# Cross-attention and feed-forward on one core: group 0's divisions on ScalarE, output weights' loads ahead of sums, first weights loaded by column halves

## The chip, the cores and the metric

The kernel runs on one core of one Trainium2 chip. The metric is the time of one execution on the device, in microseconds (us). The core has five engines that run their own queues of instructions in order: TensorE (PE in the profile; PEld is its load of weights), VectorE (DVE), ScalarE (ACT), GpSimd (POOL) and SyncE (SP). Transfers are issued from SyncE's, ScalarE's and GpSimd's queues.

## The reference, cut to what matters

There are 8 batches of 128 rows, a width of 512, 32 heads of width 128, and an inner feed-forward width of 1376. All is float32.

```
h     = rmsnorm(layernorm(x)) * ln_weight          # 8 x 128 x 512
q     = h @ w_q.T;  k = ctx @ w_k.T;  v = ctx @ w_v.T     # 32 heads of 128
score = softmax(where(mask, q k^T + position_bias, -inf)); 0 where masked
att   = (score @ v), heads side by side            # 8 x 128 x 4096
x     = x + layernorm(x) + att @ w_out.T
g     = layernorm(x)
x     = x + (silu((g @ Wg.T) * ag) * ((g @ Wu.T) * au)) @ Wd.T * ad
```

Two sequences in the softmax matter here: the exponentials with their row sums, and the division of each row by its sum.

## The kernel before

**Groups, batches, and products with fewer multiplications.** The 32 heads are worked in 8 groups of 4 (`NG`, `GH`), so a group's weights are 512 columns (`GW`). Most matrix products are done in a scheme of seven products of half-sized blocks in place of eight (`seven`, `inner`, `four`): the operands are split into quarters, sums of quarters are formed ahead (`sums_a`, `sums_b`, `combine_rows`, `token_sums`), TensorE multiplies, and ScalarE copies or VectorE adds each product into its result. So each weight needs four sums on GpSimd before all of its products can run, but the first two products read weights that are in no sum.

**The start.** The first group's weights of k and v (`wk0`, `wv0`) and the transposed context (`ctx_sb`) come from HBM; each tile holds 4 chunks of 128 rows. Lines 152 to 162 issue them: chunks 2 and 3 of k and of the context's first 512 tokens one by one, then v, then the rest in halves (`load_part`), ScalarE's queue and SyncE's queue in parallel. The context's other 512 tokens come last, in two parts. `first_kv` (566) then runs the products of k and v of group 0 in the order of 570 to 589: two products of k's blocks (number 2), two of v's, then number 1 of each, then those that read sums. `ctx_sums(0)` to `ctx_sums(3)` are the token sums on VectorE and GpSimd. In the same loop (682) x is normalised on VectorE and ScalarE. Then the queries of all groups are projected and stored to HBM (741 to 772).

**The groups.** From line 888 on, group g's attention runs batch by batch, while the k and v of the next group are projected between the batches (`later_kv`). `probabilities` (495) does a batch of a group: 4 matmuls of scores into one bank (`sc`, one buffer); VectorE adds the masked bias that GpSimd has made (`masked_bias`, 490), takes the rows' maxima and negates them (506 to 510); ScalarE takes 4 exponentials with sums (515); VectorE inverts the sums (522, 523) and multiplies (526), writing the columns in another order, so that every fourth element of `s` is read. `transpose_p` (533) turns the result by a VectorE transposition of 32x32 blocks and a way through HBM on SyncE's queue. Three batches later `attend` (547) multiplies it by v, and ScalarE copies the product out and stores it to HBM (556, 557).

Where an engine is wrapped in `InOrder`, its instructions keep the order of the program (all such have line 62 in the profile). Otherwise a scheduler may set them in another order. Group 0 is in order for batches 0 to 3, group 7 throughout.

**The last group** (line 900 on). There is no next group, so TensorE works on the output projection meanwhile: in pass b it does batch b's scores, an older batch's product with v, and the output products of group b-1 for rows of batches 0 and 1 (`out_products`, `out_product`). For these, VectorE forms sums of the attended rows (`att_sums`, in `between`), and GpSimd sums of the output weights (`sums` in `load_wo`). `load_wo(g)` issues the weights' load on GpSimd's queue where g > 2, and returns the function that does the sums. In a pass GpSimd first makes the masked bias of batch b+2 (which waits for the division of batch b-1, whose tile it takes over), then does the sums of the weights whose load was issued at the end of the pass before (930), and at the end of the pass the next load is issued (987, 988). Group 7's weights go into two tiles of their own (791, 792). After the loop, TensorE finishes group 7's output products (1000), begins those of the next two batches' rows (1001), and so on to the residual, the second norm and the feed-forward part.

Of the kernel before, what the change touches and what calls it, by code (L numbers as in the profile page):

```python
# [17 lines left out]
P = 128  # L18
BS = 32
# [47 lines left out]
def xattn_ffn_kernel(  # L67
# [19 lines left out]
    nc = tc.nc  # L87
# [5 lines left out]
    GH = 4  # L93
    NG = H // GH
    GW = GH * P
# [5 lines left out]
    HW = GW // 2  # L101
# [41 lines left out]
    wk0 = wpool.tile([P, DC, GW], F32, tag="w", name="wk0")  # L143
    wv0 = wpool.tile([P, DC, GW], F32, tag="w", name="wv0")

    def load_part(eng, t, src, fh, cols=slice(None)):
        eng.dma_start(
            t[:, bass.ts(fh, HC), cols],
            src[bass.ts(fh, D // 2), cols].rearrange("(c p) n -> p c n", p=P),
        )  # L150

    g0 = slice(0, GW)
    for c in (2, 3):
        nc.scalar.dma_start(wk0[:, c], wkT[bass.ts(c, P), g0])
        nc.sync.dma_start(ctx_sb[:, c, :512], ctxT[bass.ts(c, P), :512])
    for c, eng in ((2, nc.scalar), (3, nc.sync)):
        eng.dma_start(wv0[:, c], wvT[bass.ts(c, P), g0])
    load_part(nc.scalar, wk0, wkT[:, g0], 0)
    load_part(nc.sync, ctx_sb, ctxT, 0, slice(0, 512))
    load_part(nc.scalar, wv0, wvT[:, g0], 0)  # L160
    for fh in (1, 0):
        load_part(nc.sync, ctx_sb, ctxT, fh, slice(512, T))
    kv_w = {0: (wk0, wv0)}
# [1 line left out]
    for b in range(B):  # L165
        nc.sync.dma_start(x_in[b // 2][:, b % 2, :], x[b])

    vector, gpsimd, scalar, sync = (
        InOrder(tc, e) for e in (nc.vector, nc.gpsimd, nc.scalar, nc.sync)
    )  # L170
# [324 lines left out]
    def probabilities(g, b, qT, kT, pb, between=None, s=None, ahead=None):  # L495

        cols = bass.ts(b, S)
        n = f"{g}_{b}"
        if s is None:
            s = masked_bias(gpsimd, g, b, pb)  # L500
        sc = ps.tile([P, GH, S], F32, tag="sc", name=f"sc_{n}")
        for j in range(GH):
            tensor.matmul(  # L503
                sc[:, j, :], qT[:, j, bass.ts(b % 2, S)], kT[j][:, cols], start=True, stop=True
            )
        vector.tensor_tensor(s, sc, s, ALU.add)
        mx = small.tile([P, GH], F32, tag="mx", name=f"mx_{n}")
        vector.tensor_reduce(mx, s, AX.X, ALU.max)
        nmx = small.tile([P, GH], F32, tag="nmx", name=f"nmx_{n}")
        vector.tensor_scalar(nmx, mx, FLOOR, -1.0, ALU.max, ALU.mult)  # L510
        sm = small.tile([P, GH], F32, tag="sm", name=f"sm_{n}")
        if ahead:
            ahead()
        for j in range(GH):
            scalar.activation(  # L515
                s[:, j, :], s[:, j, :], AF.Exp,
                bias=nmx[:, j : j + 1], accum_out=sm[:, j : j + 1],
            )
        if between:
            between()  # L520
        ri = small.tile([P, GH], F32, tag="ri", name=f"ri_{n}")
        vector.tensor_scalar_max(ri, sm, TINY)
        vector.reciprocal(ri, ri)

        p = work.tile([P, GH, S], F32, tag="p", name=f"p_{n}", bufs=1)
        vector.tensor_tensor(  # L526
            p.rearrange("q h (j r) -> q h j r", r=BS), s.rearrange("q h (r j) -> q h j r", r=BS),
            ri.unsqueeze(2).unsqueeze(3).to_broadcast([P, GH, 4, BS]), ALU.mult,
        )
        return p  # L530
# [151 lines left out]
    for n, _ in enumerate(first_kv()):  # L682
        if n in moments_at:
            pair[moments_at[n]] = norm1_moments(moments_at[n])
        if n in scales_at:
            b = scales_at[n]
# [6 lines left out]
        if n in turns_at:  # L693
            b = turns_at[n]
# [14 lines left out]
    scalar = nc.scalar  # L709
# [31 lines left out]
    for g in range(NG):  # L741
# [4 lines left out]
        w, heads = combine_rows(f"q{g}", q_w.pop(g)) if g else rows_q, []  # L746
# [26 lines left out]
    gpsimd = nc.gpsimd  # L773
# [114 lines left out]
    for g in range(NG):  # L888
        kT, v = kvs.pop(g)
        pb = biases.pop(g)  # L890
        if g + 1 < NG:
            biases[g + 1] = load_bias(g + 1)
        if g + 2 < NG:
            kv_w[g + 2] = load_kv(g + 2)
        if g == 0:
            products = later_kv()
        if g == NG - 2:
            wo_later = Later()
            load_wo(2)(wo_later)
        if g == NG - 1:  # L900
            tensor, vector = InOrder(tc, nc.tensor), InOrder(tc, nc.vector)
            fetched, next_fetched = {}, {}
            gpsimd, sync, wo_sums = InOrder(tc, nc.gpsimd), InOrder(tc, nc.sync), None
            biased = [masked_bias(gpsimd, g, k, pb) for k in range(2)]

            bulk = InOrder(tc, nc.scalar)
            come[1, 0] = load_att(1, 0, bulk)
        for b in range(B):
            if (g, b) == (NG - 2, B - 1):
                come = {(0, 0): load_att(0, 0, nc.sync)}  # L910
            if b % 2 == 0:
                qT = ahead.pop((g, b // 2))
                at = todo.index((g, b // 2)) + 2
                if at < len(todo):
                    ahead[todo[at]] = load_queries(*todo[at], nc.sync if g + 1 < NG else bulk)

            if (g, b) == (0, 0):
                tensor = kv_tensor = InOrder(tc, nc.tensor)
                vector, scalar, gpsimd = (
                    InOrder(tc, e) for e in (nc.vector, nc.scalar, nc.gpsimd)  # L920
                )
                done = next(products) + next(products)
            if g == NG - 1:


                if b + 2 < B:
                    biased.append(masked_bias(gpsimd, g, b + 2, pb))
                for _ in range(2):
                    wo_later.next(gpsimd)
                if wo_sums:  # L930
                    wo_sums = wo_sums(gpsimd)

                def between():
                    if b == 0:
                        next(products)
                    fetched[b] = att_sums(b, 0, come.pop((b, 0)), vector)

                p = probabilities(g, b, qT, kT, pb, between, biased.pop(0))
            elif g == 0 and b < 4:
                def one():  # L940
                    nonlocal done
                    done += next(products)

                if b == 0:
                    biased = [masked_bias(gpsimd, g, k, pb) for k in range(2)]
                biased.append(masked_bias(gpsimd, g, b + 2, pb))
                p = probabilities(g, b, qT, kT, pb, one, biased.pop(0), one)
            elif g == 0 and b < 6:
                p = probabilities(g, b, qT, kT, pb, s=biased.pop(0))
            else:  # L950
                p = probabilities(g, b, qT, kT, pb)
                if g == NG - 2:
                    for _ in range((0, 1, 1, 1, 1, 2, 2, 2)[b]):
                        wo_later.next(InOrder(tc, nc.gpsimd))
            pend.append((g, b, transpose_p(g, b, p), v))
            advance(3)

            if g == NG - 1:
                while next(products, None):
                    pass  # L960
            else:
                while done < due(g, b):
                    done += next(products)
            if (g, b) == (NG - 2, 2):

                sums.close()
                wos = pools(outp)("wosA", 2, side="right", reuse_waits="tile")
                load_wo(0)(wo_later)
                load_wo(1)(wo_later)
            if (g, b) == (0, 3):  # L970
                tensor, vector, scalar = nc.tensor, nc.vector, nc.scalar
                kv_tensor = tensor
            if (g, b) == (1, B - 1):
                gpsimd = nc.gpsimd
            if g == NG - 1:
                if b == 0:
                    proj.close()
                    wos = pools(outp)("wosB", 2, reuse_waits="tile")

                    first_banks = [  # L980
                        pl.tile([P, 2, HW], F32, tag=tag, name=f"m{k}_0")
                        for k, (pl, tag) in enumerate(2 * [(ps_mm, "mm")] + 2 * [(ps_b, "i")])
                    ]
                    first_out = out_products(0, list(range(NG)), first_banks, fetched)
                n = (b + 2) % B, (b + 2) // B
                come[n] = load_att(*n, bulk)
                if b < NG - 3:
                    wo_sums = load_wo(b + 3)
                if b:
                    next(first_out)  # L990
                if b + 2 >= B:
                    next_fetched[n[0]] = att_sums(*n, come.pop(n), gpsimd)


    scalar = InOrder(tc, nc.scalar)
# [15 lines left out]
    vector, gpsimd = nc.vector, nc.gpsimd  # L1011
# [78 lines left out]
    scalar = nc.scalar  # L1090
# [120 lines left out]
    for i in range(NP):  # L1211
# [9 lines left out]
        if i == 0:  # L1221
            wd = load_down()

            gpsimd = InOrder(tc, nc.gpsimd)
# [162 lines left out]
```

## Time and profile before

| | us |
|---|---|
| median of 3 runs | 1087.78 |
| lowest and highest | 1086.01, 1088.52 |
| the profiled execution | 1089.21 |
| its span, first to last instruction | 1087.4 |
| TensorE busy | 1074.8 |
| VectorE busy | 659.4 |
| ScalarE busy | 331.7 |
| GpSimd busy | 442.5 |
| mean granted TensorE clock | 0.999 |

How to read it: the profile is one execution, with times in us from its first instruction. In a timeline each line is a start, a duration, the engine, the line of the kernel, the operation, output<-inputs, shapes and a count; in brackets stands how long the engine was idle before it and what ended that. TensorE's float32 matmuls appear as two records for each instruction. In the list of waits each line is the engine and what it did, what it waited for, the total in us, the times and the longest. In the chain of waits each line is a start, a duration and what was being done or waited for. The groups of instructions have the count and, after the bar, the busy time in us, the mean of one in ns, and the idle time before them. In five-us stretches, VectorE is busy 4.37 us from 15 to 20 and 4.86 us from 20 to 25, and not at all from 10 to 15. From 240 to 320, which is nearly all of group 0, TensorE is busy 75.94 us of 80, VectorE 66.63 and ScalarE 36.16.

### The profile page before, as it was taken

How to read it: one execution, taken by the hardware profiler on the slowest of the kernel's cores; microseconds unless marked ns; L12 is line 12 of the kernel's file. 1: busy time of each engine (PE TensorE's matmuls, PEld its weight loads, DVE VectorE, ACT ScalarE, POOL GpSimd, SP SyncE). 2: the span in 40 equal slices, each digit the busy share in tenths (PEclk: the TensorE clock that was granted, in tenths of full speed). 3: DMA queues.
4: the chain of work that ended last, by engine and by line, in shares of the span. 5: the costliest groups of instructions: out<-in, count | busy, mean ns of one | idle time of the engine just before them, and what ended most of it. 6: DMA issues, size and time to landing. Idle time of an engine off the chain costs nothing.

```text
span 1087.4 us, 13761 instructions
## 1 busy us (share of the span) xinstructions
PE 1074.8 (99%) x4802; PEld 790.5 (73%) x4802; DVE 659.4 (61%) x1219; ACT 331.7 (31%) x902; POOL 442.5 (41%) x488
## 2 busy tenths in 40 slices
PE   9999999998999999999999999999999999999998
PEld 5656666556869788887879778978888864444787
DVE  4653443447888888888787767854544242544732
ACT  2633223214544444444444343311000012233100
POOL 6233554624565545555551444561000317920010
PEclk9999999999999999999999999999999999999999
DMA  9613344453755465454645657673442622110011
GB/s 290 194 53 117 116 172 170 161 207 122 243 185 194 161 199 182 135 199 153 217 165 189 214 183 225 237 263 110 173 136 78 194 80 77 39 39 1 1 39 39
DMA packets 124692, 161.80 MB, mean 149 GB/s; under 512 B 15600, under 2 KB 77296, under 8 KB 124624
## 3 DMA queue, kind: packets, MB, share of 16 engines
q1 hardware_dynamic: 110208, 129.73, 36.1%
q10 hardware_dynamic: 12544, 24.38, 6.3%
q0 software_dynamic: 1872, 6.82, 2.0%
q8 instruction: 38, 0.62, 0.2%
q14 instruction: 30, 0.25, 0.1%
HBM read 104.81 MB, written 56.10 MB: 148 GB/s over the span
## 4 chain that ended last, share of the span: by engine, by line
PE 86%; DVE 7%; DMA 3%; issue 2%; ACT 2%; POOL 0%; SPq 0%; ACTq 0%; DVEq 0%; POOLq 0%
PE mm_f L1229 11%; PE mm_q L453 10%; PE m L834 9%; PE mm_v L474 8%; PE mm_k L453 8%; PE d L1308 6%; PE i_q L402 6%; PE m L62 5%; PE i_v L415 5%; PE i_k L402 4%; PE av L551 4%; PE sc L503 4%; PE mm_v L62 2%; PE mm_k L62 1%; PE mm_q L62 1%
## 5 line engine op out<-in xcount | busy, mean ns | idle before, releaser
L515 ACT ACTIVATE s<-s,nmx 128x128 f32<-128x128 f32 x240 | 93.4, 390 | 69.5 <-DVE nmx L510 51.8
L492 POOL TENSOR_TENSOR s<-pb,mneg 128x512 f32<-128x512 f32 x40 | 50.8, 1271 | 128.5 <-DVE p L526 110.4
L397 DVE TENSOR_TENSOR q<-q,i_q 128x512 f32<-128x512 f32 x98 | 49.9, 550 | 82.1 <-PE i_q L402 81.7
L556 ACT COPY aT<-av 128x512 f32<-128x512 f32 x60 | 35.1, 585 | 144.9 <-PE av L551 113.9
L526 DVE TENSOR_TENSOR p<-s,ri 128x512 f32<-128x512 f32 x52 | 64.2, 1235 | 1.4
L503 PEld LDWEIGHTS sc<-k,q 128*128 128x128 f32 x416 | 54.0, 192 | 8.3 <-issue 6.7
L376 ACT COPY q<-mm_q 128x512 f32<-128x512 f32 x56 | 31.4, 587 | 93.8 <-PE mm_q L453 66.6
L453 PE MATMUL mm_q<-hT,wq 128*128 128x512 f32 x128 | 58.5, 592 | 0.0
L62 POOL TENSOR_TENSOR s<-pb,mneg 128x512 f32<-128x512 f32 x24 | 30.4, 1270 | 66.9 <-DVE p L526 41.0
L474 PE MATMUL mm_v<-wv,ctx_sb 128*128 128x256 f32 x240 | 56.2, 380 | 0.7 <-ACT v L345 0.7
L453 PE MATMUL mm_q<-hT,S_q 128*128 128x512 f32 x120 | 55.9, 592 | 0.0
L503 PE MATMUL sc<-k,q 128*128 128x128 f32 x416 | 55.4, 275 | 0.0
L551 PE MATMUL av<-pT,v 128*128 128x128 f32 x416 | 55.0, 275 | 0.0
L474 PE MATMUL mm_v<-S_v,ctx_sb 128*128 128x256 f32 x232 | 54.7, 380 | 0.3 <-ACT v L376 0.2
L453 PE MATMUL mm_k<-ctx_sb,wk 128*128 128x512 f32 x112 | 52.6, 593 | 0.0
L62 POOL TENSOR_TENSOR S_q<-wq 128x512 f32<-128x512 f32 x8 | 10.1, 1268 | 104.2 <-ACT wq L62 104.2
L397 DVE TENSOR_TENSOR v<-v,i_v 128x512 f32<-128x512 f32 x84 | 43.9, 541 | 11.6 <-PE i_v L415 11.1
L551 PEld LDWEIGHTS av<-pT,v 128*128 128x128 f32 x416 | 50.6, 192 | 0.1
L62 PE MATMUL m<-wo,a 128*128 128x256 f32 x200 | 49.3, 382 | 1.3 <-DMA wo<-in_woT_dram 0.9
L474 PEld LDWEIGHTS mm_v<-wv,ctx_sb 128*128 128x128 f32 x240 | 44.8, 190 | 6.5 <-ACT v L345 0.9
L453 PE MATMUL mm_k<-ctx_sb,S_k 128*128 128x512 f32 x104 | 48.6, 593 | 0.0
L834 PE MATMUL m<-wo,a 128*128 128x256 f32 x200 | 48.4, 379 | 0.0
(327 smaller groups left out, 2465.2 us busy)
## 6 DMA issues: line engine op xcount, KB each, us to landing
queries<-q SPq DMA_DIRECT2D x32, 512.0 KB, 3.9
turned<-tt SPq DMA_DIRECT2D x64, 256.0 KB, 2.8
pT<-turned SPq DMA_DIRECT2D x64, 256.0 KB, 3.0
att<-aT ACTq DMA_DIRECT2D x64, 256.0 KB, 2.9
q<-queries SPq DMA_DIRECT2D x30, 512.0 KB, 5.1
a<-att SPq DMA_DIRECT2D x23, 512.0 KB, 4.3
wq<-in_wqT_dram SPq DMA_DIRECT2D x8, 1024.0 KB, 6.9
wk<-in_wkT_dram SPq DMA_DIRECT2D x7, 1024.0 KB, 5.4
```

The lines of the kernel that those rows point to most:

```text
L62: return self.tc.keep_in_program_order(getattr(self.engine, op)(*args, **kw))
L397: vector.tensor_tensor(to, to, out, ADD)
L402: kv_tensor.matmul(out, a[n][i], b[n][i], start=first, stop=True, skip_group_check=True)
L453: kv_tensor.matmul(out, w[i][:, c, bass.ts(t, P)], src[i][:, c, :], start=(first and c == 0), stop=(c == HC - 1), skip_group_check=True,)
L474: kv_tensor.matmul(out[:, bass.ts(k, HW)], src[i][:, c, bass.ts(2 * t + k, S)], w[i][:, c, :], start=(first and k == 0 and c == 0), stop=( ...
L503: tensor.matmul(sc[:, j, :], qT[:, j, bass.ts(b % 2, S)], kT[j][:, cols], start=True, stop=True)
L515: scalar.activation(s[:, j, :], s[:, j, :], AF.Exp, bias=nmx[:, j : j + 1], accum_out=sm[:, j : j + 1],)
L526: vector.tensor_tensor(p.rearrange("q h (j r) -> q h j r", r=BS), s.rearrange("q h (r j) -> q h j r", r=BS), ri.unsqueeze(2).unsqueeze(3). ...
L551: tensor.matmul(av[:, j, :], v[b // 2][:, b % 2, bass.ts(j, P)], pT[:, :, j, :], start=True, stop=True,)
L834: tensor.matmul(m[n], sa[n][:, c, :], wo_t[g][n][:, c, :], start=(g == order[0] and c == 0 and PRODUCTS.index(n) % 2 == 0), stop=(g == ord ...
L1229: nc.tensor.matmul(out, ws[t][n][:, c, :], h2_t[n][:, :, c, :], start=(first and c == 0), stop=(c == HC - 1), skip_group_check=True,)
L1308: nc.tensor.matmul(out, lhs, rhs, start=bank not in started, stop=(i == NP - 1 or n == 8), skip_group_check=True,)
```

## The change

Three things are changed.

1. The first weights of k and v are loaded by halves of their columns: the left 256 columns of the chunks that the first products read come first (k's by chunk, then v's, then the other row halves), and both right halves follow in one transfer each. The transfers of the context keep their order, but on SyncE's queue v's left half of rows 0 to 255 and v's right half now stand ahead of its last two.
2. In group 0 the division is done by four ScalarE multiplications, one for each head of the group, in place of one VectorE operation. The reading and writing order stays.
3. In the last group, the load of group b+3's output weights is issued in pass b after the bias, ahead of the sums of those of group b+2. It was issued at the end of the pass. As the first load (group 3) is still issued at the end of pass 0, the sums begin in the same pass as before.

```
-    g0 = slice(0, GW)
+    left, right = slice(0, HW), slice(HW, GW)
     for c in (2, 3):
-        nc.scalar.dma_start(wk0[:, c], wkT[bass.ts(c, P), g0])
+        nc.scalar.dma_start(wk0[:, c, left], wkT[bass.ts(c, P), left])
         nc.sync.dma_start(ctx_sb[:, c, :512], ctxT[bass.ts(c, P), :512])
-    for c, eng in ((2, nc.scalar), (3, nc.sync)):
-        eng.dma_start(wv0[:, c], wvT[bass.ts(c, P), g0])
-    load_part(nc.scalar, wk0, wkT[:, g0], 0)
+    load_part(nc.scalar, wv0, wvT, 1, left)
     load_part(nc.sync, ctx_sb, ctxT, 0, slice(0, 512))
-    load_part(nc.scalar, wv0, wvT[:, g0], 0)
+    load_part(nc.scalar, wk0, wkT, 0, left)
+    load_part(nc.sync, wv0, wvT, 0, left)
+    for eng, w, src in ((nc.scalar, wk0, wkT), (nc.sync, wv0, wvT)):
+        eng.dma_start(w[:, :, right], src[:, right].rearrange("(c p) n -> p c n", p=P))
     for fh in (1, 0):
         load_part(nc.sync, ctx_sb, ctxT, fh, slice(512, T))
...
         p = work.tile([P, GH, S], F32, tag="p", name=f"p_{n}", bufs=1)
+        if g == 0:
+            for j in range(GH):
+                scalar.mul(
+                    p[:, j].rearrange("q (j r) -> q j r", r=BS),
+                    s[:, j].rearrange("q (r j) -> q j r", r=BS), ri[:, j : j + 1],
+                )
+            return p
         vector.tensor_tensor(
...
-            gpsimd, sync, wo_sums = InOrder(tc, nc.gpsimd), InOrder(tc, nc.sync), None
+            gpsimd, sync = InOrder(tc, nc.gpsimd), InOrder(tc, nc.sync)
...
-                if wo_sums:
-                    wo_sums = wo_sums(gpsimd)
+                if 0 < b < NG - 3:
+                    wo_todo.append(load_wo(b + 3))
+                if b and wo_todo:
+                    wo_todo.pop(0)(gpsimd)
...
-                if b < NG - 3:
-                    wo_sums = load_wo(b + 3)
+                if b == 0:
+                    wo_todo = [load_wo(b + 3)]
```

## The prediction

> **What bounds the kernel now.** I read the page's busy shares, then who waited for whom on TensorE, then the timeline in the three places that the diff touches.
>
> ```profile
> PE 1074.8 (99%) x4802; PEld 790.5 (73%) x4802; DVE 659.4 (61%) x1219; ACT 331.7 (31%) x902; POOL 442.5 (41%) x488
> ```
>
> TensorE is busy for 1074.8 of 1087.4 us, and no part of the change removes a matmul. So the most that it can win is idle time of TensorE, 12.6 us and the little that pipelined durations hide. Its longest waits, in us:
>
> ```profile
> PE i_k L62 <- DVE k L62: 2.0, 1, 2.0
> PE i_k L402 <- POOL s L62: 1.0, 1, 1.0
> PE m L62 <- POOL wo L62: 0.9, 1, 0.9
> PE m L62 <- DMA wo<-in_woT_dram: 0.9, 2, 0.7
> ```
>
> The first two lie in group 0, the last two where the output weights of group 7 are first used. "POOL s" is a wrong name: that matmul starts as VectorE ends its sum of the bank before it (260.12, below).
>
> **Output weights earlier: what it removes.** GpSimd's timeline in group 7:
>
> ```profile
> 705.41 0.77 POOL L62 DMA_DIRECT2D wo<-in_woT_dram  x1
> ...
> 719.78 1.44 POOL L62 DMA_DIRECT2D wo<-in_woT_dram  x2
> ...
> 726.11 1.27 POOL L62 TENSOR_TENSOR wo<-wo 128x512 f32<-128x512 f32 x1 [3.58 <-DMA wo<-in_woT_dram]
> ```
>
> and TensorE's at the same place:
>
> ```profile
> 724.29 1.05 PE L62 MATMUL av<-pT,v 128*128 128x128 f32 x8
> 726.02 1.13 PE L62 MATMUL m<-wo,a 128*128 128x256 f32 x4 [0.67 <-DMA wo<-in_woT_dram]
> ...
> 737.96 1.05 PE L62 MATMUL av<-pT,v 128*128 128x128 f32 x8
> ```
>
> Each load is issued behind the sums of the one before, so GpSimd alternates between sums (5.5 us) and waiting for a load, some 14 us per batch, while TensorE takes 7.83 (677.31, 685.14, 692.97). The last load, 719.78, comes too late. After the scores' product of 724.29 ends (725.18), 44 matmul records follow up to 737.96; at 0.216 each (28 took 6.05) they need 9.5 us and took 12.78: 3.27 lost.
>
> Changed, the load of group b+3 stands ahead of the sums of b+2. From the trace's durations: bias of batch 4 679.4, load of 5 680.7, sums of 4 681.4-687; the next pass waits for the division of batch 2 (below), loads 6 at 689.6, sums 5 to 696; then bias, both loads of 7 at 698.4-699.9, sums 6 to 705.6; bias 7, sums 7 from 707.5 (a load takes about 8.4) to 712.6. TensorE wants them at 725.2: 12 us to spare. What the loads of 7 wait for (output product 1, scores of batch 3) ends by 686. GpSimd's next work, the sums of the attended rows, then starts near 718 in place of 731.7; wanted at 731. What follows (last attended copies, first residual, the 0.3 us wait for att at 760.9) hangs on TensorE's last scores' product and moves along. Gain 3.2.
>
> What speaks against it is contention on VectorE:
>
> ```profile
> 688.63 1.38 DVE L62 TENSOR_TENSOR S_a<-S_a,a 128x256 f32<-128x256 f32 x1
> ...
> 691.35 2.10 DVE L62 TENSOR_TENSOR S_a<-a,S_a 128x256 f32<-128x256 f32 x1
> ```
>
> These sums take 0.42 when GpSimd is still (697.47). In passes 1, 3 and 5 GpSimd's sums ran beside them and a pass of VectorE took 9.0 (670.90 to 679.88); in passes 2 and 4 it took 5.5. Now GpSimd's sums come in every pass. The Trainium skill, "SBUF — State Buffer", Who interferes with whom, says that a VectorE operation with two SBUF inputs and a GpSimd one that reads SBUF exclude each other for whole instructions. Taken at its worst, all five GpSimd operations of a pass (5 x 1.27) fall before VectorE's: 5.5 + 6.35 = 11.9 a pass, 4 over TensorE's 7.83, and after four passes nothing of the gain is left. The row gives 9.0-9.2, and GpSimd's bias waits for VectorE's division, which keeps them in step. Then S_a of batch 3 ends near 695.7, wanted at 696.48; of batch 4 near 702.8, wanted at 704.31; from batch 5 VectorE recovers. I take no stall; the ends are 0 and 2 us.
>
> **Divisions of group 0 on ScalarE.**
>
> ```profile
> 258.37 1.08 DVE L62 TENSOR_TENSOR p<-s,ri 128x512 f32<-128x512 f32 x1
> 259.49 0.71 DVE L62 STREAM_TRANSPOSE tt<-p 128x512 f32<-128x512 f32 x1
> 260.12 0.65 DVE L62 TENSOR_TENSOR k<-k,i_k 128x512 f32<-128x512 f32 x1
> ```
>
> ```profile
> 260.92 1.53 PE L402 MATMUL i_k<-t_c,s_k 128*128 128x256 f32 x6 [0.98 <-POOL s L62]
> 264.47 1.56 PE L62 MATMUL i_k<-t_c,s_k 128*128 128x256 f32 x6 [2.02 <-DVE k L62]
> ```
>
> Eight VectorE divisions of 1.08-1.82 go; 32 ScalarE multiplications of 128x128 come. As the changed instructions stand, no table load is added. In batches 0 to 2 the order on VectorE stays: reciprocal, transposition of p, sums of k. The transposition now waits for ScalarE, and the sums that TensorE waits for stand behind it. So what counts is not VectorE's freed 1.08 but whether four multiplications are done sooner than one division. Nearest rows (groups of instructions, by shape):
>
> ```profile
> L62 ACT ACTIVATE wq<-wq,lnw_sb 128x512 f32<-128x512 f32 x32 | 23.1, 726 | 8.3 <-DMA wq<-in_wqT_dram 8.3
> L62 ACT ACTIVATE hn<-x,nm,rr 128x512 f32<-128x512 f32 x8 | 10.4, 1320 | 0.5 <-DVE nm L62 0.5
> L62 ACT ACTIVATE s<-s,nmx 128x128 f32<-128x128 f32 x16 | 6.2, 390 | 11.4 <-DVE nmx L62 11.4
> ```
>
> hn reads every fourth element, as the new multiplication does: 0.6 over wq for 512 elements, 0.15 for 128. An exponential holds ScalarE for 0.30 before its accumulator read. So 0.45 each, 1.8 for four, and 0.1 from engine to engine: 1.9 against the 1.12 from division to transposition. VectorE's queue is 0.8 later in each of batches 0, 1, 2, a little of which its waits absorb: TensorE is 2.2 behind at the product of 268.49. Also, in batch 0 two copies of k stand behind the multiplications and hold a product some 0.9, which the same later waits swallow. Bounds: 0.30 each (no price for the stride) gives 0.2 a batch; 0.54 (0.39 + 0.15, nothing overlapped) gives 1.1.
>
> From batch 3 on, VectorE works on scores ahead of the transposition and has 1.1-1.8 less per batch. Its two later stalls of TensorE, before 301.53 (0.55 and 0.15 in slower starts) and 306.91 (0.27 and 0.25), go: -1.3. ScalarE must carry exponentials 1.64, multiplications 1.8, copy of av 0.59, two copies of v 1.1: 5.1 a batch, against TensorE's pace of 4.8, 4.8, 5.8, 6.3 (scores at 272.50, 277.30, 282.11, 287.91, 294.25): just carried. Sum: 2.2 - 1.3 = +0.9. At 0.30: about -1.0; at 0.54: 3.4 - 1.3 + 1.2 (ScalarE's surplus over three batches) = +3.3.
>
> **First weights by halves.** TensorE's early waits for data (0.8 inside the first products of k, 0.3 before v at 9.18) mostly go: the left halves are all that these products read. But the chain of the start goes on through
>
> ```profile
> 6.29 9.32 DMA ctx_sb<-in_ctxT_dram
> ```
>
> the last part of the context, landing at 15.61. From there VectorE is busy without a gap (token sums, k and v, moments) and ScalarE's copies of k stand in order behind a square root that waits for it, which is what TensorE waits for at 27.10 and 29.35. That part comes after the same 4 MB as before; only halves are exchanged ahead of it, and SyncE's queue alone draws 386 GB/s (15 to 19 us). So TensorE arrives half a microsecond sooner and waits that much longer: -0.1. The halves go in pieces of 1 KB. The skill, "DMA: Bandwidth & Descriptors", Why small descriptors are slow, charges some 3 cycles per packet over 32-byte beats; my estimate by it is 70 in place of 67 cycles for 2 KB, so 4.5% on 2 MB, 0.24 us later. The row for such pieces here (wu, 512 KB, around 903 us) runs at 369-403 GB/s, no slower than 2 KB pieces at 386: 0. Ends: -0.5 and +0.6.
>
> **Sum.** The profiled execution took 1089.21, 1.8 around its span of 1087.4. -3.2 + 0.9 - 0.1 = -2.4: 1086.8. The median of the runs, 1087.78, is 1.43 below it: 1085.4.
>
> **Rivals.**
> 1. Multiplications near 0.30: group 0 gains 1.0, total -4.3: 1083.5. For: the exponentials' 0.30. Against: hn. 0.17.
> 2. Slower, by ScalarE's queue in group 0 alone. At 0.65 each: 3 x (2.7 - 1.12) - 1.3 + 3 x (5.93 - 5.1) = +5.9, less 3.3: 1090.4. It turns from gain to loss at 0.54. For: ScalarE is full there, and TensorE needs its copies. Against: no row of 128 elements is over 0.40. 0.18.
> 3. The output weights' gain isn't had: VectorE's contention puts a wait of 2 to 3 us in place of the one removed, in batches 3 and 4. -0.3 + 0.9 - 0.1: 1088.3. For: 0.8 us of margin. Against: GpSimd waits for VectorE in each pass. 0.20.
>
> **The numbers.** Likeliest 0.45, at 1085.4, own range 1083.9-1087.2. A measurement tells about 0.2%, 2.2 us: faster is below 1085.6, slower above 1089.95. Faster: rival 1 and somewhat over half of the likeliest, 0.42. Slower: most of rival 2, a little of 3: 0.16. Same: 0.42. The range leaves out the upper half of rival 2 and the lower of 1: 1083.0 to 1089.9.
>
> **What would show it.** Right: no wait for wo near 725, the scores' product of 737.96 3.2 sooner relative to group 7's start; ScalarE multiplications of 0.45; TensorE's waits in group 0 before 270 grown by 2, those at 301 and 306 gone; TensorE at 29.35 as before. Wrong: S_a of batches 3 or 4 named in TensorE's waits; multiplications over 0.54; the last context part landing away from 15.6.

## The result, and the profile after

| | before | after |
|---|---|---|
| median, us | 1088.15 (1086.01 to 1090.69, 6 runs) | 1093.12 (1092.13 to 1095.0, 6 runs) |
| ratio after/before | | 1.0043, 95% interval 1.0029 to 1.0056 |
| profiled execution, us | 1089.21 | 1093.86 |
| its span, us | 1087.4 | 1091.8 |
| mean granted TensorE clock | 0.999 | 0.996 |

The changed kernel is slower, by 5.0 us. The forecast was 1085.4 with a range of 1083.0 to 1089.9: wrong in its sign.

The busy shares of the page, after:

```profile
PE 1076.7 (99%) x4802; PEld 793.5 (73%) x4802; DVE 655.7 (60%) x1211; ACT 345.7 (32%) x934; POOL 442.8 (41%) x488
```

ScalarE has 32 instructions more and VectorE 8 fewer, as the diff says. Who waited for whom on TensorE, after (what waited, for what, us in total, times, longest):

```profile
PE i_k L62 <- DVE k L62: 2.0, 1, 2.0
PE av L560 <- DMA pT<-turned: 1.9, 1, 1.9
PE mm_k L62 <- ACT k L62: 1.8, 3, 0.8
PE i_k L404 <- POOL s L62: 1.3, 1, 1.3
...
PE sc L62 <- DVE s L62: 1.0, 2, 0.7
PE mm_v L62 <- DMA wv<-in_wvT_dram: 0.9, 1, 0.9
PE mm_k L62 <- DVE ctx_sb L62: 0.7, 1, 0.7
```

The two waits for `wo` are gone. In their place stand four kinds that were not in the list before: for `pT` (the turned probabilities in group 0), for `s` (the sum of scores and bias in group 7), and, at the start, for v's weights (`wv`) and for `ctx_sb` (the token sums).

**Where the time is lost.** I compare the start of the same four matmuls on TensorE in the two traces. Each row says how much later TensorE stands there than in the kernel before, and how much of that came in since the row above:

| TensorE's instruction | before | after | later by | new in this stretch |
|---|---|---|---|---|
| product of k, end of the start | 29.35 | 31.02 | 1.67 | +1.67 |
| scores after group 0 | 318.17 | 324.37 | 6.20 | +4.53 |
| first scores of group 7 | 662.51 | 668.19 | 5.68 | -0.52 |
| product with v after group 7's output weights | 737.96 | 742.07 | 4.11 | -1.57 |
| end of the span | 1087.4 | 1091.8 | 4.4 | +0.3 |

So the start and group 0 lose, and group 7 wins, but half of what it was to win. The experiments take the three parts one by one, and then ask of each what it is made of. Their table by stretches, made in the same way (us against the one profiled execution of the kernel before):

| kernel | start | group 0 | groups 1 to 6 | group 7 | rest |
|---|---|---|---|---|---|
| halves_only | +2.11 | +0.52 | +0.20 | -1.15 | +0.8 |
| rows_new_order | +1.85 | +0.50 | -0.48 | -0.87 | +0.4 |
| divisions_only | -0.05 | +3.04 | -0.20 | -0.96 | +0.4 |
| wo_only | +0.18 | +0.53 | +0.16 | -1.60 | +0.3 |
| div_p_first | -0.03 | +6.24 | +0.34 | -0.87 | +0.4 |
| div_from_5 | +0.07 | +1.09 | +0.13 | -3.28 | +0.3 |
| div_wv2_late | +0.05 | +2.25 | -0.15 | -0.90 | +0.8 |
| div_to_2 | +0.05 | +2.63 | -0.16 | -3.09 | +0.7 |
| wv2_load_late | +0.07 | -0.23 | +0.29 | -3.28 | +1.2 |
| wo_last_early | +0.20 | +0.75 | -0.34 | -3.28 | +0.6 |
| wo_two_early | +0.21 | +0.87 | +0.60 | -1.15 | +0.5 |
| wv2_late_wo_last | +0.25 | -0.74 | +0.43 | -2.08 | +0.7 |

A stretch that an edit doesn't touch shows how far one execution stands from another: group 0 by up to 0.9 us, group 7 by -0.9 to -3.3 (more on that below). Whether a whole kernel gained is therefore read from the medians, and only the mechanism from the traces.

### The profile page after: what moved, and what is told of

The parts are those of the page before. It is cut to its first block, busy times and chain, and to the rows that moved or that the text cites. A ratio compares the mean times of both kernels' runs of the same rounds, so it can differ in the third digit from the quotient of the medians.

```text
span 1091.8 us, 13790 instructions
## 1 busy us (share of the span) xinstructions
PE 1076.7 (99%) x4802; PEld 793.5 (73%) x4802; DVE 655.7 (60%) x1211; ACT 345.7 (32%) x934; POOL 442.8 (41%) x488
## 4 chain that ended last, share of the span: by engine, by line
PE 86%; DVE 8%; DMA 3%; ACT 1%; issue 1%; ACTq 0%; SPq 0%; POOL 0%; DVEq 0%; POOLq 0%
PE mm_f L1241 11%; PE mm_q L455 10%; PE m L843 9%; PE mm_v L476 8%; PE mm_k L455 8%; PE d L1320 6%; PE i_q L404 6%; PE i_v L417 5%; PE i_k L404 4%; PE m L62 4%; PE av L560 4%; PE sc L505 4%; PE mm_v L62 2%; DVE S_a L62 2%; PE mm_k L62 1%
## 5 line engine op out<-in xcount | busy, mean ns | idle before, releaser
L535 DVE TENSOR_TENSOR p<-s,ri 128x512 f32<-128x512 f32 x48 | 58.9, 1226 | 1.3
```

What stands on the lines that cost most here:

```text
L535: vector.tensor_tensor(p.rearrange("q h (j r) -> q h j r", r=BS), s.rearrange("q h (r j) -> q h j r", r=BS), ri.unsqueeze(2).unsqueeze(3). ...
```

## Experiments

### The three parts, each alone

Three kernels hold one part of the change each, with its lines as in the diff above. The fourth keeps the start's new order and queues, but loads whole rows of 2 KB:

```
-    for c, eng in ((2, nc.scalar), (3, nc.sync)):
-        eng.dma_start(wv0[:, c], wvT[bass.ts(c, P), g0])
-    load_part(nc.scalar, wk0, wkT[:, g0], 0)
+    load_part(nc.scalar, wv0, wvT[:, g0], 1)
     load_part(nc.sync, ctx_sb, ctxT, 0, slice(0, 512))
-    load_part(nc.scalar, wv0, wvT[:, g0], 0)
+    load_part(nc.scalar, wk0, wkT[:, g0], 0)
+    load_part(nc.sync, wv0, wvT[:, g0], 0)
```

First weights by halves, alone:

> Kernel before with the first weights' loads by halves alone. The prediction's step: the start ends where it did (TensorE's product that waits for ScalarE's copy of k at 29.35), median -0.1: 1088.0. What the trace of the changed kernel says: pieces of 1 KB took 51 ns where pieces of 2 KB took 87, so the last part of the context lands about 1.1 later (16.7 for 15.6), GpSimd's sums of the first weights start at 13.7 for 12.0, and TensorE stands at 31.0 for 29.35: +1.7, 1089.8.

The new order with whole rows:

> Kernel before with the loads of the start in the changed kernel's order and on its queues, but whole rows of 2 KB in place of halves. If the size of the pieces is the cause, the last part of the context lands at 15.6 as before and the time is within 0.3 of before (1088.1). If the order or the queues are the cause, it lands near 16.7 and the time is +1.7 as with the halves.

Divisions of group 0 on ScalarE, alone:

> Kernel before with group 0's divisions on ScalarE alone. The prediction's step: +0.9, 1089.0. What the trace of the changed kernel says: VectorE's queue later by 0.7 in each of batches 0 to 2 (TensorE +2.1), a wait of 1.9 for pT near 288, since SyncE's queue has the load of wv2 ahead of batch 3's store, two later stalls gone (-1.6): +2.4, 1090.5, with TensorE's clock at full; up to +4.5 (1092.6) where it is halved twice for 3.4 us behind these waits.

Output weights' loads ahead of the sums, alone:

> Kernel before with the output weights' loads ahead of the sums alone. The prediction's step: -3.2, 1084.9. Its third rival: the gain lost again, 1088. What the trace of the changed kernel says: the 3.3 near 725 go, but VectorE takes 9.4 per batch beside GpSimd's sums and TensorE waits for it at the scores' products of batches 6 and 7, 1.7 in all: -1.6, 1086.5.

| kernel | median, us | range, runs | against before | ratio, 95% |
|---|---|---|---|---|
| before | 1088.31 | 53 runs | | |
| halves_only | 1089.79 | 1088.21 to 1091.99, 22 | +1.48 | 1.0017 (1.0010 to 1.0025) |
| rows_new_order | 1089.30 | 1088.06 to 1092.79, 20 | +0.99 | 1.0016 (1.0008 to 1.0025) |
| divisions_only | 1091.34 | 1089.66 to 1092.80, 10 | +3.03 | 1.0028 (1.0017 to 1.0039) |
| wo_only | 1088.54 | 1087.76 to 1089.44, 14 | +0.23 | 1.0004 (0.9995 to 1.0013) |

The three parts add up to 4.7 us, and the whole change costs 5.0: they hardly act on each other. Two of them lose and the third gives nothing. The fifth column is the difference of the medians; the ratio is taken from all executions and can stand apart from it (for rows_new_order 1.0016 is 1.7 us).

**What the start shows.** VectorE's first token sum, in the changed kernel and in halves_only:

```profile
16.71 1.88 DVE L62 TENSOR_TENSOR ctx_sb<-ctx_sb 128x1024 f32<-128x1024 f32 x1 [6.38 <-DMA x<-in_x_dram]
```

```profile
16.82 2.20 DVE L62 TENSOR_TENSOR ctx_sb<-ctx_sb 128x1024 f32<-128x1024 f32 x1 [6.34 <-DMA ctx_sb<-in_ctxT_dram]
```

Before, it started at 15.63 and took 1.28. It starts 1.1 later, because the last part of the context lands at 16.7 in place of 15.6 (in the changed kernel it was issued at 6.1 and took 10.6; the bracket names the load of x), and it takes 0.6 to 0.9 more. By its end VectorE is 1.68 and 2.1 behind, and TensorE at its 29.35 is 1.67 and 2.11 behind: the chain that the prediction named passes the whole delay on.

Why the context lands late is seen from what the DMA engines moved between 9 and 12 us. The changed kernel, then whole rows in the same order:

```profile
DMA packets 1047, 1.04 MB, mean 346 GB/s; under 512 B 32, under 2 KB 1047, under 8 KB 1047
```

```profile
DMA packets 603, 1.16 MB, mean 386 GB/s; under 512 B 38, under 2 KB 38, under 8 KB 603
```

The kernel before had 386 GB/s with 598 packets there, and halves_only 346 with 1046. One packet took 51 ns at 1 KB and 87 at 2 KB (medians). So pieces of 1 KB ran 10% slower. With whole rows the context landed at 15.9, only 0.3 late.

But the order alone costs nearly as much, and its expectation was missed. TensorE of rows_new_order:

```profile
11.00 3.72 PE L62 MATMUL mm_v<-wv,ctx_sb 128*128 128x256 f32 x16 [1.21 <-DMA wv<-in_wvT_dram]
...
31.20 1.98 PE L62 MATMUL mm_k<-ctx_sb,wk 128*128 128x512 f32 x4 [0.30 <-ACT k L62]
```

The first product of v starts 1.82 later than before (9.18), since the value weights that it reads now stand behind k's on one queue, and TensorE is 1.85 behind at 31.20. The halves repair this wait (9.66) and pay for it with the context's landing and, as shown next, with that of k's right half.

**Why VectorE's sum takes longer.** GpSimd's sums of k's weights also start later. VectorE's first sum and GpSimd's first and fourth sum, before, and then GpSimd's in the changed kernel:

```profile
15.63 1.28 DVE L62 TENSOR_TENSOR ctx_sb<-ctx_sb 128x1024 f32<-128x1024 f32 x1 [5.66 <-DMA ctx_sb<-in_ctxT_dram]
```

```profile
12.01 1.26 POOL L62 TENSOR_TENSOR S_k<-wk 128x512 f32<-128x512 f32 x1 [8.34 <-DMA wk<-in_wkT_dram]
...
15.79 2.25 POOL L62 TENSOR_TENSOR S_k<-wk,S_k 128x512 f32<-128x512 f32 x1
```

```profile
13.68 1.27 POOL L62 TENSOR_TENSOR S_k<-wk 128x512 f32<-128x512 f32 x1 [10.02 <-DMA wk<-in_wkT_dram]
...
17.47 2.25 POOL L62 TENSOR_TENSOR S_k<-wk,S_k 128x512 f32<-128x512 f32 x1
```

In all 14 profiled executions VectorE's first sum took between 1.23 and 2.20, but ended 1.11 to 1.14 after GpSimd had begun its next sum. So it is held until the GpSimd sum beside it is over. In the changed kernel and in halves_only it meets the same GpSimd sum as before, the third, and GpSimd is 1.67 and 2.11 late: that is the whole delay of VectorE (1.68 and 2.1) and of TensorE (1.67 and 2.11). GpSimd waits for the weights of k, whose last part landed at 13.6 in the changed kernel and at 11.9 before. Its first sum reads the right columns of k alone (`combine_rows`), which the change loads last. The late context decides which of GpSimd's sums VectorE meets: in rows_new_order (15.9, GpSimd 1.83 late) it is the second, and VectorE ends only 0.6 behind. By an estimate from these times, a context landing at 15.6 would have made VectorE meet the second sum in the changed kernel too, and end 0.5 behind. So both loads count, the context's and that of k's right half.

### Divisions: the queue in front of p, or the bytes beside it

In the profile of divisions_only, TensorE waits 1.84 us for `pT`, as it does in the changed kernel. SyncE's queue in the changed kernel:

```profile
279.56 0.38 SPq L130 DMA_DIRECT2D wv<-in_wvT_dram  x1
280.04 0.53 SPq L274 DMA_DIRECT2D turned<-tt  x1
280.62 2.93 SPq L875 DMA_DIRECT2D q<-queries  x2
286.79 0.37 SPq L279 DMA_DIRECT2D pT<-turned  x1
```

Before, batch 3's `turned` went out at 274.87, ahead of the value weights (275.82, 1 MB), and its way back was issued at 276.89, 2.0 later. Now the weights go first, the store takes 6.7 to land in place of 2.0, and the way back is issued 6.7 after it. Two kernels move the load of those weights, both with all divisions of group 0 on ScalarE. div_p_first keeps the order of before, batch 3's p ahead of the load:

```
-            vector, nc.sync, n, p.rearrange("q h (j r) -> q h j r", r=BS), (pT, slice(None))
+            vector, sync if g == 0 and b == 3 else nc.sync, n, p.rearrange("q h (j r) -> q h j r", r=BS), (pT, slice(None))
...
         if g + 2 < NG:
-            kv_w[g + 2] = load_kv(g + 2)
+            if g == 0:
+                wk2 = load_w("wk2", wkT[:, bass.ts(2, GW)])
+            else:
+                kv_w[g + 2] = load_kv(g + 2)
...
             pend.append((g, b, transpose_p(g, b, p), v))
+            if (g, b) == (0, 3):
+                kv_w[2] = wk2, load_w("wv2", wvT[:, bass.ts(2, GW)], sync)
```

div_wv2_late issues it behind batch 7's p (same edit, its tile allocated ahead, batch 7 in place of 3).

> All of group 0's divisions on ScalarE, as in the changed kernel, but batch 3's store and load of p stand ahead of the load of wv2 on SyncE's queue, as before the change. If the queue is what held pT, TensorE's wait of 1.8 near 288 goes and about 2.3 of the 3.0 that the divisions alone cost: 1089.0. If ScalarE is simply too full in batches 3 to 5, the wait stays, under another name, and the time is 1091.

> All of group 0's divisions on ScalarE, group 2's value weights loaded after batch 7's p. If the 1 MB beside the stores and loads of p is what holds pT, the waits for pT of 1.8 to 2.7 go and what is left is VectorE's queue in batches 0 to 2 (+2.1) less the two later stalls (-1.3): +0.8 on before, 1089.1, in place of 1091.3. If ScalarE's own queue is too full: 1091.

| kernel | median, us | range, runs | against before | ratio, 95% |
|---|---|---|---|---|
| div_p_first (before 1088.22) | 1094.03 | 1091.56 to 1095.50, 5 | +5.8 | 1.0057 (1.0043 to 1.0071) |
| div_wv2_late (before 1087.97) | 1090.21 | 1088.28 to 1092.57, 18 | +2.2 | 1.0025 (1.0018 to 1.0032) |

The theory that the place in the queue alone makes the wait falls. With batch 3's p in front, that batch is in time, but the wait comes one batch later and is longer, in TensorE's list of waits for div_p_first:

```profile
PE av L558 <- DMA pT<-turned: 2.7, 1, 2.7
```

There batch 4's store took 4.1 to land and its way back 5.8, beside 1 MB of value weights, a load of queries and one of the bias. (Behind this wait the clock was halved for a while, as told at the end, which makes another 1.7 of the 6.24 in the table of stretches.) With the load out of the way (div_wv2_late) no wait for `pT` is left. So p is slow while other bytes are on the move at the same time. But +2.2 remains of +3.0, with intervals that overlap: the wait for `pT` is not the main part.

What takes its place in div_wv2_late is a wait for ScalarE. TensorE, and then ScalarE ahead of it:

```profile
277.51 1.16 PE L558 MATMUL av<-pT,v 128*128 128x128 f32 x8 [0.45 <-ACT aT L62]
...
286.80 1.16 PE L558 MATMUL av<-pT,v 128*128 128x128 f32 x8 [0.70 <-ACT aT L563]
```

```profile
275.22 1.76 ACT L62 ACTIVATE p<-s,ri 128x128 f32<-128x128 f32 x4 [0.67 <-DVE ri L62]
276.89 0.56 ACT L62 COPY aT<-av 128x512 f32<-128x512 f32 x1
...
282.48 1.79 ACT L528 ACTIVATE p<-s,ri 128x128 f32<-128x128 f32 x4 [1.21 <-DVE ri L523]
...
286.19 0.56 ACT L563 COPY aT<-av 128x512 f32<-128x512 f32 x1
```

The copy of the product with v (`aT`) stands behind four multiplications, the second time also behind exponentials, and TensorE needs the copied bank.

### Which batches cost

Two kernels use ScalarE for a part of group 0's batches only, `if g == 0 and b < 3:` and `if g == 0 and b >= 5:`.

> Group 0's divisions on ScalarE in batches 0 to 2 alone; TensorE's and SyncE's orders as before. The step of the prediction by itself: four multiplications (1.76) and two hops between engines in place of one division (1.08) make VectorE 0.7 later in each batch: TensorE +2.1 at the product of 268.5 and after it, the stalls before 301.5 and 306.9 as before: +2.1, 1090.4. If later slack swallows it: 1088.5.

> Group 0's divisions on ScalarE for batches 5 to 7 alone; TensorE's and SyncE's orders are then those of before. If the loss lies in batches 0 to 2 (VectorE's transposition waits for four multiplications) and in SyncE's queue, neither is there, and the stalls before 301.5 and 306.9 go: -1.3, 1087.0. If ScalarE is too full in batches 5 to 7: no gain, 1088.3 or later.

| kernel | median, us | range, runs | against before | ratio, 95% |
|---|---|---|---|---|
| div_to_2 (before 1087.97) | 1089.85 | 1088.61 to 1092.68, 21 | +1.9 | 1.0017 (1.0009 to 1.0024) |
| div_from_5 (before 1088.22) | 1088.69 | 1087.55 to 1091.72, 13 | +0.5 | 1.0011 (1.0002 to 1.0019) |

Batches 0 to 2 alone cost most of it. In div_to_2 TensorE waits twice for k; the first wait was there before (2.02), and the second is new:

```profile
266.01 1.56 PE L62 MATMUL i_k<-t_c,s_k 128*128 128x256 f32 x6 [2.01 <-DVE k L62]
270.77 0.70 PE L62 MATMUL i_k<-t_c,wk 128*128 128x256 f32 x2 [0.58 <-DVE k L62]
```

Batches 5 to 7 on ScalarE give no gain, although the two later stalls that the prediction wanted to remove lie there. In the trace of div_from_5 these stalls are gone, but two waits for `pT` (2.16 and 0.70) stand ahead of them.

Set side by side, TensorE's scores in group 0 show where each delay comes in (us later than before, each kernel's delay of the start taken off):

| scores at, before | after | divisions_only | div_wv2_late | div_to_2 |
|---|---|---|---|---|
| 255.86 | 1.04 | 1.02 | 1.03 | 1.11 |
| 272.50 | 2.96 | 2.14 | 2.16 | 2.24 |
| 277.30 | 2.97 | 2.87 | 2.88 | 2.25 |
| 287.91 | 6.23 | 4.39 | 3.37 | 2.20 |
| 294.25 | 6.09 | 4.60 | 3.59 | 2.73 |
| 318.17 | 4.53 | 3.04 | 2.25 | 2.63 |

By 272.50 all have the 2.1 to 2.2 of batches 0 to 2 (the 0.8 more in the changed kernel is a matter of the clock, told at the end). With ScalarE multiplying on, 0.7 comes in before 277.30 and, in divisions_only, 1.5 with the wait for `pT` before 287.91; without that wait the second wait for ScalarE brings 0.5. From 294.25 on the freed VectorE gives back 1.6 and 1.3. In div_to_2 there is little of that (three waits for `pT` of 0.26 to 0.43), and the end is about the same.

### Is the load of the value weights worth moving by itself?

wv2_load_late is the kernel before with that load behind batch 7's p.

> Kernel before with one load moved: group 2's 1 MB of value weights leaves SyncE's queue after batch 7's p (near 300) in place of between batch 3's store and load of p (275.8). If this load is what makes batch 3's p land late (its load from DRAM took 5.6 in the profile of before and 8.1 in that of the run with divisions from batch 5 on, where others take 2.6 to 2.8), p lands in about 3 and no execution waits for it: median -0.5 to -1, 1087.5. If the lateness has another cause: 1088.3.

Measured 1087.64 (1086.44 to 1089.09, 13 runs) beside 1087.97: 0.9993 (0.9983 to 1.0003), no difference that can be told. The traces do show what the load does to p. Beside it the way back of batch 3's p took 5.6 us in the profile of before, 5.8 to 6.2 in six others that keep this order (halves_only, rows_new_order, wo_only, wo_last_early, wo_two_early, div_to_2), and 8.1 in div_from_5. With the load moved it took 2.9, here and in wv2_late_wo_last. In the three kernels with the load moved TensorE has no wait for `pT` in group 0; ten of the other eleven traces have one or more. Among those that divide batch 3 on VectorE, as before, the longest is in div_from_5:

```profile
285.41 1.13 PE L558 MATMUL av<-pT,v 128*128 128x128 f32 x8 [2.16 <-DMA pT<-turned]
```

But where the divisions are those of before, these waits make only 0.5 us on average (six executions, 0 to 1.1), too little for the medians to show.

### Output weights: fewer loads ahead

wo_last_early puts only the last loads (group 7's, pass 4) ahead of the sums and leaves the others at the end of the pass, and wo_two_early those of groups 6 and 7. The edit of wo_last_early (wo_two_early has 3 in place of both 4s):

```
-            gpsimd, sync, wo_sums = InOrder(tc, nc.gpsimd), InOrder(tc, nc.sync), None
+            gpsimd, sync, wo_todo = InOrder(tc, nc.gpsimd), InOrder(tc, nc.sync), []
...
-                if wo_sums:
-                    wo_sums = wo_sums(gpsimd)
+                if 4 <= b < NG - 3:
+                    wo_todo.append(load_wo(b + 3))
+                if b and wo_todo:
+                    wo_todo.pop(0)(gpsimd)
...
-                if b < NG - 3:
-                    wo_sums = load_wo(b + 3)
+                if b < 4:
+                    wo_todo.append(load_wo(b + 3))
```

> The output weights' loads stay behind the sums, as before, but for the last one (group 7's two), which goes ahead of the sums of group 6: one step won once in place of sums in every batch. If VectorE beside GpSimd's sums in every batch is what gave the gain back, TensorE has no wait for VectorE at a scores' product and none for wo: -3, 1085.3. If the gain at 725 is not to be had (sums of group 7 then end near 726.6, TensorE wants the first at 726): -1 to -2, 1086.8.

> As the run with the last load early, but the last two (groups 6 and 7) go ahead of the sums. GpSimd's sums then lie in three batches running, 700 to 721; VectorE's last scores' sum that TensorE waits for is done by 712, wanted at 716: no wait, -3, 1085.3. If contention already shows with three batches: a wait for VectorE at the last scores' product, -2 to -2.5, 1086.

Measured: wo_last_early 1087.40 (1086.83 to 1090.81, 13 runs), 0.9997 (0.9989 to 1.0006); wo_two_early 1088.55 (1086.81 to 1093.11, 21 runs), 1.0008 (0.9998 to 1.0017), beside 1088.22. In wo_last_early's trace TensorE waits neither for `wo` nor for `s`, and still the median is only 0.8 lower, inside its interval. So even without VectorE's wait the gain is far from 3.2.

wo_two_early's profile has a wait of 1.89 for `pT` at 705.43. The likely reason is in the edit: where it begins, one load still goes at the end of a pass and the next at the head of the following pass, so that 2 MB travel at once, beside p on its way back (issued at 693.32; KB, us to landing):

```profile
692.60 0.77 POOL L62 DMA_DIRECT2D wo<-in_woT_dram  x1
...
694.60 0.77 POOL L62 DMA_DIRECT2D wo<-in_woT_dram  x1
```

```profile
pT<-turned SPq DMA_DIRECT2D x1, 256.0 KB, 12.0
```

In the kernel before, beside one load, this took 9.3 and came in time. In wo_last_early two loads leave at 704.12 and 706.12, and p took 11.1 beside them, just in time. In wv2_late_wo_last, with the same two loads, a store of p beside them took 7.6, and TensorE waits 0.96 for that `pT` at 718.41. These are single executions; no run takes the two loads apart.

Why so little is to be had at all: the wait that was to be removed isn't the same in every execution. Nine profiled executions have group 7 as before. Of each I took the gap from the product with v (724.29 in before) to the next but its undisturbed length of 10.39, and the median time of the loads of `wo`:

| execution | load, us | TensorE lost, us |
|---|---|---|
| before | 8.4 | 3.28 |
| halves_only | 8.3 | 2.13 |
| divisions_only | 8.0 | 2.31 |
| div_wv2_late | 7.9 | 2.37 |
| div_p_first | 7.8 | 2.41 |
| rows_new_order | 7.7 | 2.41 |
| div_to_2 | 6.9 | 0.19 |
| wv2_load_late | 6.6 | 0 |
| div_from_5 | 6.4 | 0 |

The line of the loads, before and in div_from_5 (count, KB each, us from issue to landing):

```profile
wo<-in_woT_dram POOLq DMA_DIRECT2D x4, 1024.0 KB, 8.4
```

```profile
wo<-in_woT_dram POOLq DMA_DIRECT2D x4, 1024.0 KB, 6.4
```

The mean loss is 1.7 us. The profile of before was the worst of the nine. How much of such a loss reaches the end of the kernel in an average execution was not measured: the interval of wo_last_early, which has neither wait, ends at a gain of 1.2.

### Both small gains together

wv2_late_wo_last joins wv2_load_late and wo_last_early.

> The same, and the last output weights' load ahead of group 6's sums. The candidate for a kernel faster than both: -1.5, 1086.7, with no wait for wo and none for pT of batch 3. If the two gains are noise of the executions: 1088.

Measured 1086.77 (1085.12 to 1091.29, 14 runs) beside 1087.97: 0.9991 (0.9980 to 1.0002). It has the lowest median of all kernels here, 1.2 us below, but its interval includes no change.

## Why the prediction was wrong

The forecast was 7.7 us too low. Its three terms account for 7.1: +1.6 at the start (+1.5 for -0.1), +2.1 for the divisions (+3.0 for +0.9), +3.4 for the output weights (+0.2 for -3.2). Another 0.4 is the median of before, which was taken as 1087.78 and came out at 1088.15.

**Output weights: "Gain 3.2".** The mechanism was right. GpSimd's timeline after has the loads ahead of the sums and no wait for them:

```profile
694.61 1.27 POOL L62 TENSOR_TENSOR s<-pb,mneg 128x512 f32<-128x512 f32 x1 [1.82 <-DVE p L62]
695.83 0.77 POOL L62 DMA_DIRECT2D wo<-in_woT_dram  x1
696.62 1.28 POOL L62 TENSOR_TENSOR T_o<-wo 128x512 f32<-128x512 f32 x1
...
705.25 1.44 POOL L62 DMA_DIRECT2D wo<-in_woT_dram  x2
```

Two steps failed.

- The size. "3.27 lost" was read from one execution, and the loads that made it were the slowest of nine. 1.7 was to be had on average (0 to 3.28).
- "I take no stall", and "from batch 5 VectorE recovers". Rival 3's mechanism came, with another last link. VectorE in a pass, after:

```profile
695.14 0.65 DVE L62 TENSOR_TENSOR s<-sc,s 128x512 f32<-128x512 f32 x1
695.82 0.69 DVE L62 TENSOR_REDUCE mx<-s 128x4 f32<-128x512 f32 x1
696.54 1.39 DVE L62 TENSOR_SCALAR nmx<-mx 128x4 f32<-128x4 f32 x1
698.29 1.38 DVE L62 TENSOR_TENSOR S_a<-S_a,a 128x256 f32<-128x256 f32 x1
699.60 1.48 DVE L62 TENSOR_TENSOR a<-a 128x256 f32<-128x256 f32 x1
701.00 1.49 DVE L62 TENSOR_TENSOR S_a<-a,S_a 128x256 f32<-128x256 f32 x1
...
704.56 0.65 DVE L62 TENSOR_TENSOR s<-sc,s 128x512 f32<-128x512 f32 x1
```

From one sum of scores to the next it is 9.42 us, not 9.0 to 9.2. Sums over 256 elements take 1.4 to 1.5 in place of 0.42, and the negation of the maxima (`nmx`), four elements, takes 1.39 in place of some 0.2: it was not in the count. (In the kernel before, `nmx` took 0.91, 0.53 and 0.60 in the three passes with GpSimd's sums.) The wait of GpSimd's bias for the division (`p`, 1.82 above), which was argued to keep the two in step and so harmless, holds GpSimd to VectorE's 9.42 as well, so that its sums meet VectorE in every pass and nothing recovers. TensorE's pass is 7.83, so VectorE falls back by 1.6 a pass until its margin is used up. Then TensorE waits, not for S_a, which I had watched, but for the bank of the scores, which VectorE has to read before the next are written:

```profile
715.12 1.16 PE L62 MATMUL sc<-k,q 128*128 128x128 f32 x8 [0.65 <-DVE s L62]
723.75 1.16 PE L62 MATMUL sc<-k,q 128*128 128x128 f32 x8 [0.35 <-DVE s L62]
```

In all that cost 1.7: TensorE's delay grows from 5.68 to 7.39 between the first scores of group 7 and the product at 731.68, and falls to 4.11 where the wait for `wo` had been. In wo_only's trace it is 1.7 too. 1.7 paid for 1.7 had on average: nothing, which fits what wo_only measured (+0.2). The Trainium skill's rule ("SBUF — State Buffer", Who interferes with whom), at its worst 11.9 a pass, would have made a pass far too long, and the row of before (9.0) made it a little too short. The measured pass lies near the row; it was the conclusion drawn from it that failed.

**Divisions: "2.2 - 1.3 = +0.9".** The sizes were right. Four multiplications took 1.76 (predicted 1.8):

```profile
260.76 1.76 ACT L62 ACTIVATE p<-s,ri 128x128 f32<-128x128 f32 x4 [0.51 <-DVE ri L62]
```

From the end of the reciprocal to the transposition each batch got 0.7 longer (predicted 0.8); TensorE was 2.1 to 2.2 behind at the scores of 272.50 (predicted 2.2), and div_to_2 measured 1.9. The "-1.3" in later batches came too: 1.6 in divisions_only. What failed is the sentence "just carried". ScalarE's 5.1 us a batch against a pace of 4.8 to 6.3 was right as a sum, but it left no room for the order in which they stand: a copy of `aT` behind the multiplications came late and cost 0.7 (in div_wv2_late a second one cost 0.5). Rival 2 had this mechanism, but let it begin at 0.54 for a multiplication; it came at 0.44 (1.76 / 4). And the transfer of a p that comes later was not priced: it now meets 1 MB of value weights, which cost 1.5 in the trace of divisions_only (0.8 between the medians of divisions_only and div_wv2_late, not clear of noise). So 0.7 + 1.5 ate what VectorE gave back. (The bound at 0.30 is added up wrongly: 3 x 0.2 - 1.3 is -0.7, not -1.0, which takes rival 1 from 1083.5 to 1083.8.)

**First weights: "only halves are exchanged ahead of it", "-0.1".** The chain was right from VectorE's first sum on, the sign wrong. Two steps failed.

- The landing of the context. For pieces of 1 KB I took the row of `wu` (369 to 403 GB/s), which lay in another place under another load. At the start they ran at 346 against 386, and the context landed 1.1 later. The skill's rule ("DMA: Bandwidth & Descriptors", Why small descriptors are slow) spoke against the change and had the right sign; its estimate of 4.5% and 0.24 us was half of the rate that was lost (10%) and under a third of the delay that goes with the pieces (0.8 of the 1.1; the rest is the new order's).
- "From there VectorE is busy without a gap". VectorE's first sum hangs not on the context alone but also on GpSimd's sums, and these on k's right half, which the change puts last. That half was put at nothing. It came 1.7 later, and TensorE's 1.67 at 31.02 is this delay.

## What to carry to other kernels

A stall that ends on a transfer is worth its mean over executions, not what one profile shows: look for its spread in other traces before counting on it. Where two engines hold each other up, as VectorE and GpSimd do here, moving the one's work out of a wait moves it beside the other's; add up that other engine's pass with every overlapped instruction in it, the small ones too, and compare it with the pace of the engine that sets the end. Work shifted to an idle engine is charged twice: for what waits for it, and for what stands behind it in that engine's queue. And before a load is put last because one engine needs it late, look who else reads it: the half of k's weights that TensorE could wait for was the first that GpSimd read.

## What the runs showed of the hardware

**The TensorE clock is halved for 3.41 us after a stretch of little work.** The changed kernel in stretches of 3.41 us, counted from the start of a drop (us from:to, length, TensorE busy and its instructions, granted clock, DMA share, GB/s):

```profile
264.90:268.31 3.41, 1.40 (x7) 1.00 0.28 83
268.31:271.72 3.41, 3.41 (x14) 0.50 0.00 0
...
288.79:292.20 3.41, 1.51 (x12) 1.00 1.08 337
292.20:295.61 3.41, 3.41 (x10) 0.50 0.70 211
```

After 1.40 and 1.51 us of work in 3.41 (0.41 and 0.44), the next stretch runs at half the clock. The same wait in the kernel before left more work in its stretch, and the clock stayed:

```profile
260.29:263.70 3.41, 1.53 (x6) 1.00 0.29 99
263.70:267.11 3.41, 2.64 (x16) 1.00 0.20 59
```

In the profiled executions of all kernels here, all nine such drops inside the run follow a stretch with a busy share of 0.44 or less, and none follows one of 0.45 or more (stretches counted in steps of 3.41 us from the clock's own records). In the kernel before, 1.53 is 0.45. The Trainium skill ("TensorE: Matmul & The Clock Gate", Part 1) has the gate close after an idle window of some 3.4 us; here no window was idle. A wait of 1.9 us thus becomes a loss of 3.3, as at 287.91 in the table of group 0, where divisions_only, with a wait of the same length and no drop, lost 1.5. It isn't what made the change slow. Three executions of the changed kernel without a drop have spans of 1090.4 to 1090.9, three with one 1091.1 to 1093.1, so at most some 1 us of the 5. In the kernel before, 53 of 150 executions show a granted clock of 0.998 and have a median span of 1086.3; 94 with the full clock have 1086.35. There a drop costs nothing in the end: in halves_only TensorE is 1.5 behind at the scores of 272.50, after a drop, and 0.5 at 318.17, as the stalls that follow get shorter.

**A VectorE sum waits for the GpSimd sum beside it.** At the start VectorE's sum of 128x1024 took 1.23 to 2.20 us and ended 1.11 to 1.14 after GpSimd's next sum began, in 14 of 14 executions. In group 7 sums of 128x256 took 0.42 alone and 1.4 to 1.5 beside GpSimd's sums, and an operation on 128x4 took 0.17 alone and up to 1.39.

**One transfer's time varies.** The same load of 1 MB took 6.4 to 8.4 us (median of four) in nine executions of kernels that do not differ there. What travels beside a transfer counts as well: 256 KB of p from HBM took 2.9 us with the value weights moved away, 5.6 to 8.1 beside this 1 MB, and 11.1 and 12.0 beside 2 MB of output weights.
